# A constant of the feed-forward's last step, added to its rows on another engine and at another time

## The chip, the core and the metric

The kernel runs on one core of a Trainium2 chip. The metric is the device time of one execution in microseconds (us); it was run three times. Five engines matter: TensorE (PE; PEld is its weight load), VectorE (DVE), ScalarE (ACT), GpSimd (POOL) and SyncE (SP), whose queue here issues DMAs. Each engine takes its own instructions in order and waits for the others by semaphores.

## The reference, cut to what matters

The model has two layers of graph attention followed by a feed-forward. The change lies in the feed-forward of the first layer, 30 steps on 4096 rows of 256 channels, whose result is added to the rows it began from:

```python
def step(h, _):
    h = h + 0.01 * jnp.tanh(h)
    h = h * jax.nn.sigmoid(h)
    h = _layernorm(h, ln_w, ln_b)
    h = jnp.einsum('bsc,dc->bsd', h, W) + b
    return (h, None)
...
x = x + _L0_gnn_ref(_layernorm(x, axis=-1), adj, ...)
x = x + _L0_ffn_ref((_layernorm(x, axis=-1))[None], ...)[0]
x = x + _L1_gnn_ref(L1_gnn_t, _layernorm(x, axis=-1), adj, ...)
```

Call the rows before the feed-forward x1 and those after it x2. Then x2 is x1 plus the outcome of the 30th step.

## The kernel before

The 4096 rows are cut into 8 groups (`NG`) of 4 tiles (`G`) of 128 rows. A unit is one step of one group, so there are 240 units (`units`), and the steps of a group follow each other with seven other groups between. Between steps the kernel keeps h times 100 in an SBUF tile `y` [128, 32, 256].

A function `slot(at)` writes one turn of a software pipeline. In slot `at` the engines work on different units:

- `th` of unit `at`: ScalarE's tanh (L826), then GpSimd's add of `y` (L827). The add has an extra wait written by hand: for VectorE's `lower` instruction (L818) of the same slot, with the reason "the port that both use".
- unit `at - 2`: ScalarE's silu into `z` (L815) and the f16 part of half of it (L817); VectorE's rest of that part (L818); a DMA transpose of both f16 parts from SP's queue (L822); VectorE's statistics (L839, L841).
- unit `at - 3`: TensorE's transposes of the other half (L796), ScalarE's copy `zT` (L846), and the inverse deviation `z_rs`, which takes one small ScalarE instruction (L849) and two small GpSimd instructions (L850 with a power of -0.5, L851).
- unit `at - 4`: TensorE's matmuls into `po` (L863 in f32, L866 in f16 parts), two PSUM buffers.
- unit `at - 5`: VectorE's `po` times `z_rs` plus a constant (L803), four instructions of 128 x 256. In steps 1 to 29 the constant is `bias`; in the last it is `last`, made once at the beginning (L730) with the scale for the final result, and the outcome goes to `y` as well.
- also unit `at - 5`, in the last step only: GpSimd adds the group of `y` to the rows x1 (L877, one instruction of 128 x 1024), and SP stores the sum as x2 (L878). The first four groups stay in SBUF for the next stage in `ahead`.

```python
if units - NG <= u < units:
    g = u % NG
    t = x1.pop(g)
    nc.gpsimd.tensor_tensor(t, t, y[:, g * G : (g + 1) * G, :], OP.add)
    nc.sync.dma_start(rows_of(x2d, g), t)
```

The rows x1 are loaded again for this: groups 0 to 3 into the pool `stream` through `load`, groups 4 to 7 into four tiles `x1` of their own (L790).

The order in slots 0 to 239 is kept as written for PE, DVE, ACT and POOL (`manual_schedule`). SP is not among these engines, and the last six slots (240 to 245) and all of the next stage are ordered by the scheduler of the language, by its own estimates. It can put instructions of the next stage between the last written ones where data permits.

The next stage is `attention("g1", ...)`. Its preparation takes each group of x2: row statistics (L100, L102), 1/deviation (L104, L105), transposes (L113), a copy (L271), the products `ph` (L300), which use PSUM that `po` had, and `fs` (L314) in two halves. Groups 4 to 7 are read back from x2 in HBM by SP (L92), into the buffers of groups 0 to 3.

Of the kernel before, what the change touches and what calls it, by code (L numbers as in the profile page):

```python
# [11 lines left out]
F32 = mybir.dt.float32  # L12
# [6 lines left out]
OP = mybir.AluOpType  # L19
# [4 lines left out]
P = 128  # L24
C = 256
# [4 lines left out]
G = 4  # L30
# [16 lines left out]
def gnn_ffn_kernel(ctx: ExitStack, tc: tile.TileContext, a: dict, out: bass.AP):  # L47
    nc = tc.nc
# [3 lines left out]
    NG = NT // G  # L52
# [26 lines left out]
    x1d = dram.tile([N, C], F32, name="x1d")  # L79
    x2d = dram.tile([N, C], F32, name="x2d")  # L80
# [3 lines left out]
    def rows_of(t, g):  # L84
        return t[g * GR : (g + 1) * GR, :].rearrange("(r p) c -> p r c", p=P)

    ahead = {}
    stream = []

    def load_ahead(src, g, view=rows_of, queue=nc.sync):  # L90
        t = stream[-1].tile([P, G, C], F32, name="rows")
        queue.dma_start(t, view(src, g))  # L92
        ahead[g] = t
# [554 lines left out]
    with ExitStack() as scope:  # L648
# [8 lines left out]
        bias = one.tile([P, C], F32, name="bias")  # L657
        last = one.tile([P, C], F32, name="last")
        y = one.tile([P, NT, C], F32, name="y")
        work = scope.enter_context(tc.tile_pool(name="f_work", bufs=3))  # L660
        small = scope.enter_context(tc.tile_pool(name="f_small", bufs=6))

        x1 = {}

        def load(g, queue=nc.sync):
            if g not in ahead:
                load_ahead(x1d, g, queue=queue)
            x1[g] = ahead.pop(g)
# [3 lines left out]
        def measure(g):  # L672
            st = small.tile([P, G, 6], F32, name="x_st")
            mv = measured[g] = small.tile([P, G, 2], F32, name="x_mv")
            for r in range(G):
                nc.vector.bn_stats(st[:, r, :], x1[g][:, r, :])
            for r in range(G):
                nc.vector.bn_aggr(mv[:, r, :], st[:, r, :])

        def rate(g):  # L680

            mv = measured.pop(g)
            rs = small.tile([P, G], F32, name="x_rs")
            nc.scalar.activation(rs, mv[:, :, 1], AF.Identity, scale=1e-4, bias=eps[:, 1:])
            nc.gpsimd.tensor_tensor(rs, rs, mhalf, OP.pow)
            nm = small.tile([P, G], F32, name="x_nm")
            nc.gpsimd.tensor_tensor(nm, mv[:, :, 0], rs, OP.mult)
            nc.gpsimd.tensor_scalar(nm, nm, -1.0, None, op0=OP.mult)
            rates[g] = rs, nm

        def init(g):
            t = x1.pop(g)
            rs, nm = rates.pop(g)
            for r in range(G):
                nc.scalar.activation(
                    y[:, g * G + r, :], t[:, r, :], AF.Identity, scale=rs[:, r : r + 1], bias=nm[:, r : r + 1]
                )
# [83 lines left out]
        units = FFN_STEPS * NG  # L781
        def slot(at):
            if 0 < at and at + 3 < NG:
                load(at + 3)
            g = at - (units - NG - 4)
            if 0 <= g < NG // 2:
                load(g)
            elif NG // 2 <= g < NG:
                x1[g] = work.tile([P, G, C], F32, name="x1", bufs=NG - NG // 2)
                nc.sync.dma_start(x1[g], rows_of(x1d, g))  # L790
            u = at - 3
            if 0 <= u < units:
                z = zs.pop(u)
                pt = ps_t.tile([P, GR], F32, name="tp")
                for r in range(G):
                    nc.tensor.transpose(pt[:, r * P : (r + 1) * P], z[:, r, :P], ident)  # L796
            u = at - 5
            if 0 <= u < units:
                g = u % NG
                po, rstd = pos.pop(u), rs.pop(u)  # L800
                end = u >= units - NG
                for r in range(G):
                    nc.vector.scalar_tensor_tensor(  # L803
                        y[:, g * G + r, :],
                        po[:, r, :],
                        rstd[:, r : r + 1],
                        last if end else bias,
                        op0=OP.mult,
                        op1=OP.add,
                    )  # L810
            u = at - 2
            lower = None
            if 0 <= u < units:
                z = zs[u] = work.tile([P, G, C], F32, name="z")
                nc.scalar.activation(z, th.pop(u), AF.Silu, scale=0.01)  # L815
                z16 = work.tile([P, 2, G, P], F16, name="z16", bufs=4)
                nc.scalar.activation(z16[:, 0], z[:, :, P:], AF.Identity, scale=scale[:, :1])  # L817
                lower = nc.vector.scalar_tensor_tensor(  # L818
                    z16[:, 1], z[:, :, P:], scale[:, :1], z16[:, 0], op0=OP.mult, op1=OP.subtract
                )  # L820
                zT16[u] = work.tile([P, 2 * G, P], F16, name="zT16", bufs=4)
                nc.sync.dma_start_transpose(zT16[u], z16.rearrange("p s r c -> p (s r c)"))  # L822
            if at < units:
                g = at % NG
                th[at] = work.tile([P, G, C], F32, name="th", bufs=4)
                nc.scalar.activation(th[at], y[:, g * G : (g + 1) * G, :], AF.Tanh, scale=0.01)  # L826
                ins = nc.gpsimd.tensor_tensor(th[at], th[at], y[:, g * G : (g + 1) * G, :], OP.add)  # L827
                if lower is not None:
                    tc.add_manual_dep(
                        ins.ins,  # L830
                        lower.ins.name,
                        mybir.DependencyInfo(mybir.DependencyClass.Sync, mybir.DependencyReason.DATA),
                        reason="the port that both use",
                    )
            if 0 <= u < units:
                st = small.tile([P, G, 6], F32, name="z_st")
                mv = small.tile([P, G, 2], F32, name="z_mv")
                for r in range(G):
                    nc.vector.bn_stats(st[:, r, :], z[:, r, :])  # L839
                for r in range(G):  # L840
                    nc.vector.bn_aggr(mv[:, r, :], st[:, r, :])  # L841
                mvs[u] = mv
            u = at - 3
            if 0 <= u < units:
                zT[u] = work.tile([P, GR], F32, name="zT")
                nc.scalar.copy(zT[u], pt)  # L846

                rs[u] = small.tile([P, G], F32, name="z_rs")
                nc.scalar.activation(rs[u], mvs.pop(u)[:, :, 1], AF.Identity, bias=eps[:, :1])  # L849
                nc.gpsimd.tensor_tensor(rs[u], rs[u], mhalf, OP.pow)  # L850
                nc.gpsimd.tensor_tensor(rs[u], rs[u], under[:, int(u >= units - NG), :], OP.mult)  # L851
            if at + 2 < NG:
                rate(at + 2)
            if at + 1 < NG:
                init(at + 1)
            if at + 3 < NG:
                measure(at + 3)
            u = at - 4
            if 0 <= u < units:
                src, src16 = zT.pop(u), zT16.pop(u)  # L860
                po = pos[u] = ps_o.tile([P, G, C], F32, name="po")
                for r in range(G):
                    nc.tensor.matmul(po[:, r, :], src[:, r * P : (r + 1) * P], wT, start=True, stop=False)  # L863
                    for part in range(2):
                        for other in range(2):
                            nc.tensor.matmul(  # L866
                                po[:, r, :],
                                src16[:, part * G + r, :],
                                w16[:, other, :],
                                start=False,  # L870
                                stop=(part == 1 and other == 1),
                            )
            u = at - 5
            if units - NG <= u < units:
                g = u % NG
                t = x1.pop(g)
                nc.gpsimd.tensor_tensor(t, t, y[:, g * G : (g + 1) * G, :], OP.add)  # L877
                nc.sync.dma_start(rows_of(x2d, g), t)  # L878
                if g < NG // 2:
                    ahead[g] = t  # L880

        with tc.manual_schedule(
            engines={
# [9 lines left out]
        for at in range(units, units + 6):  # L893
            slot(at)
# [12 lines left out]
    for i in range(2):  # L907
        at = 1 + i * KC * E
# [29 lines left out]
    with ExitStack() as scope:  # L938
# [253 lines left out]
        with tc.tile_pool(name="r_ps", bufs=1, space=PSUM) as psum, tc.tile_pool(  # L1192
            name="r_pst", bufs=4, space=PSUM
# [19 lines left out]
        work = scope.enter_context(tc.tile_pool(name="m_work", bufs=3))  # L1213
# [166 lines left out]
```

## Time and profile before

| what | us |
|---|---|
| median of 3 runs (lowest, highest) | 3008.34 (3007.27, 3010.92) |
| the profiled run's own time | 3008.46 |
| its span, first to last instruction | 3006.8 |
| mean granted TensorE clock | 0.974 of full |
| GpSimd: 240 adds L827, busy (mean of one) | 568.2 (2.368) |
| GpSimd: 240 L850, busy (mean of one) | 245.7 (1.024) |
| GpSimd: 240 L851, busy (mean of one) | 96.1 (0.400) |
| GpSimd: 8 adds L877, busy | 18.8 |
| VectorE: 32 last-step L803, busy (mean of one) | 15.3 (0.476) |

The feed-forward's first L827 begins at 609.7 us and the last at 1561.7; the 32 last-step L803 begin between 1546.7 and 1581.2. Times in the views count from the first instruction of the execution. An instruction's row may begin some hundredths before its predecessor on the same engine has ended[...]. An idle time in square brackets stands before an instruction, with the engine and line that ended it.

### The profile page before, as it was taken

The numbers are of one execution on the slowest core, as the hardware profiler recorded it, in microseconds if no ns is written. First come the engines' busy times: TensorE is split into PE (matmuls) and PEld (weight loads), VectorE is DVE, ScalarE is ACT, GpSimd is POOL, SyncE is SP. The second block draws the span as 40 slices with busy tenths as digits, with TensorE's granted clock in tenths as the row PEclk, the third lists the DMA queues.
The fourth block names the chain that finished last, engine by engine and source line by source line (L and its number), as shares of the span: only waits on it lengthen the run. The fifth ranks groups of instructions, "written<-read, shape, count | busy, mean of one in ns | idle before, by whom it ended". The sixth has DMA issues, their size and how long they took to land. (4 is left out here: it accounts for less than half of the span.)

```text
span 3006.8 us, 82646 instructions
## 1 busy us (share of the span) xinstructions
PE 2813.1 (94%) x33923; PEld 2568.3 (85%) x33923; DVE 2741.0 (91%) x5766; ACT 2462.0 (82%) x3132; POOL 1173.2 (39%) x1056
## 2 busy tenths in 40 slices
PE   6899999979999999999998999999889999986996
PEld 5799999958888888888876999999789999975996
DVE  8999999989999999999998899999689999986775
ACT  5799999788888888888866999999699999963442
POOL 2000000089999999999993000000200000013663
PEclk9999999989999999999999999999999999997998
DMA  9999784143333333333343031220303132133253
GB/s 292 267 256 249 224 247 118 33 133 70 68 68 67 68 70 69 68 68 68 68 95 121 20 103 51 76 79 27 107 20 93 51 107 79 51 96 123 82 172 134
DMA packets 482899, 320.08 MB, mean 106 GB/s; under 512 B 416573, under 2 KB 443354, under 8 KB 476378
## 3 DMA queue, kind: packets, MB, share of 16 engines
q1 hardware_dynamic: 467698, 287.13, 35.6%
q0 software_dynamic: 7680, 21.51, 2.3%
q10 hardware_dynamic: 7144, 6.16, 0.6%
q8 instruction: 268, 4.39, 0.6%
q14 instruction: 109, 0.89, 0.1%
HBM read 183.00 MB, written 52.04 MB: 78 GB/s over the span
## 5 line engine op out<-in xcount | busy, mean ns | idle before, releaser
L519 PE MATMUL acc<-vals,st 128*128 128x130 f16 x12288 | 1431.1, 218 | 36.1 <-DVE u L472 27.9
L519 PE MATMUL acc<-vals,below 128*128 128x130 f16 x12288 | 1430.7, 221 | 12.6 <-DVE below L573 11.9
L461 ACT ACTIVATE st<-f1b,nf 128x1024 int8<-128x1024 f32 x1265 | 1334.2, 1142 | 29.9 <-PE acc L519 24.6
L519 PEld LDWEIGHTS <-below 128*128 128x128 fp8e4 x12288 | 1175.7, 96 | 49.4 <-issue 44.5
L519 PEld LDWEIGHTS <-st 128*128 128x128 fp8e4 x12288 | 1207.5, 98 | 9.6 <-DVE st L567 7.5
L863 PE MATMUL po<-wT,zT 128*128 128x256 f32 x1920 | 576.1, 382 | 7.4 <-ACT zT L846 7.4
L827 POOL TENSOR_TENSOR th<-th,y 128x1024 f32<-128x1024 f32 x240 | 568.2, 2368 | 27.2 <-ACT th L826 4.4
L866 PE MATMUL po<-w,zT 128*128 128x256 f16 x3840 | 577.9, 273 | 0.3 <-DMA zT<-z 0.3
L866 PEld LDWEIGHTS <-zT 128*128 128x128 f16 x3840 | 376.3, 98 | 161.6 <-DMA zT<-z 1.2
L573 DVE TENSOR_TENSOR below<-m,st 128x1024 int32<-128x1024 int32 x384 | 470.0, 1224 | 32.8 <-DVE st L567 1.3
L567 DVE TENSOR_TENSOR st<-st,m 128x1024 int32<-128x1024 int32 x384 | 467.5, 1217 | 0.2
L803 DVE SCALAR_TENSOR_TENSOR y<-po,z_rs,bias 128x256 f32<-128x256 f32 x928 | 384.4, 477 | 2.1 <-PE tp L796 0.7
L839 DVE BATCH_NORM_STATS2 z_st<-z 128x6 f32<-128x256 f32 x960 | 335.8, 413 | 0.0
L863 PEld LDWEIGHTS po<-wT,zT 128*128 128x128 f32 x1920 | 291.1, 192 | 17.4 <-ACT zT L846 9.0
L105 POOL TENSOR_TENSOR ln_rstd<-ln_rstd,mhalf 128x4 f32<-128x4 f32 x24 | 32.3, 1345 | 586.5 <-ACT acc L1033 491.8
L815 ACT ACTIVATE z<-th 128x1024 f32<-128x1024 f32 x240 | 251.2, 1047 | 8.6 <-POOL th L827 8.3
L826 ACT ACTIVATE th<-y 128x1024 f32<-128x1024 f32 x240 | 249.8, 1041 | 0.1
L850 POOL TENSOR_TENSOR z_rs<-z_rs,mhalf 128x4 f32<-128x4 f32 x240 | 245.7, 1024 | 0.0
L846 ACT COPY zT<-tp 128x512 f32<-128x512 f32 x240 | 140.4, 585 | 110.5 <-PE tp L796 110.4
L459 DVE TENSOR_SCALAR st<-f1b,nf 128x1024 int8<-128x1024 f32 x271 | 201.2, 743 | 8.4 <-PE acc L519 8.4
L436 POOL MEMSET hs<- 128x4 f32 x3 | 0.3, 101 | 491.9 <-DVE u L489 491.9
L818 DVE SCALAR_TENSOR_TENSOR z<-z,scale,z 128x512 f16<-128x512 f32 x240 | 179.4, 747 | 4.9 <-ACT z L817 4.9
(252 smaller groups left out, 2970.2 us busy)
## 6 DMA issues: line engine op xcount, KB each, us to landing
adj<-in_adj_dram SPq DMA_DIRECT2D x64, 1024.0 KB
m<-edges SPq DMA_DIRECT2D x32, 1024.0 KB
f1b<-fd SPq DMA_DIRECT2D x48, 512.0 KB
edges<-m SPq DMA_DIRECT2D x16, 1024.0 KB
y<-yd SPq DMA_DIRECT2D x16, 512.0 KB
ew<-in_L_ffn_expert_w_dram SPq DMA_DIRECT2D x18, 256.0 KB
t<-in_x_dram SPq DMA_DIRECT2D x8, 512.0 KB
old<-in_x_dram SPq DMA_DIRECT2D x16, 256.0 KB
```

The source lines that it names most:

```text
L461: nc.scalar.activation(out, f1, AF.Sign, bias=f2, scale=-1.0)
L519: nc.tensor.matmul(acc[:, i, cols], masked[part][:, at_i // TR, s, rows], v[:, cols], start=(j == 0 and part == 0), stop=(j == NT - 1 and ...
L567: nc.vector.tensor_tensor(above, above, whole, OP.bitwise_and)
L573: nc.vector.tensor_tensor(below, whole, above, OP.bitwise_xor)
L803: nc.vector.scalar_tensor_tensor(y[:, g * G + r, :], po[:, r, :], rstd[:, r : r + 1], last if end else bias, op0=OP.mult, op1=OP.add,)
L815: nc.scalar.activation(z, th.pop(u), AF.Silu, scale=0.01)
L826: nc.scalar.activation(th[at], y[:, g * G : (g + 1) * G, :], AF.Tanh, scale=0.01)
L827: ins = nc.gpsimd.tensor_tensor(th[at], th[at], y[:, g * G : (g + 1) * G, :], OP.add)
L839: nc.vector.bn_stats(st[:, r, :], z[:, r, :])
L850: nc.gpsimd.tensor_tensor(rs[u], rs[u], mhalf, OP.pow)
L863: nc.tensor.matmul(po[:, r, :], src[:, r * P : (r + 1) * P], wT, start=True, stop=False)
L866: nc.tensor.matmul(po[:, r, :], src16[:, part * G + r, :], w16[:, other, :], start=False, stop=(part == 1 and other == 1),)
```

## The change

The constant of the last step no longer comes in with VectorE's last instruction. Instead, GpSimd adds `last` to the rows x1 beforehand, one tile of 128 x 256 at a time, in 32 instructions spread over slots 40 to 220: a group every 24 slots, its four tiles at the 8th, 12th, 16th and 20th of them, each written at the end of a slot behind L851. In the last step VectorE's instruction takes these rows as its addend and writes its result over them. The eight GpSimd adds L877 go away, and the store follows VectorE's instruction directly. The lines that load the rows x1 move to one group every 24 slots from slot 32. `y` isn't written in the last step.

```diff
         def slot(at):
             if 0 < at and at + 3 < NG:
                 load(at + 3)
-            g = at - (units - NG - 4)
-            if 0 <= g < NG // 2:
-                load(g)
-            elif NG // 2 <= g < NG:
-                x1[g] = work.tile([P, G, C], F32, name="x1", bufs=NG - NG // 2)
-                nc.sync.dma_start(x1[g], rows_of(x1d, g))
+            g, part = divmod(at - 4 * NG, 3 * NG)
+            if 0 <= g < NG and part == 0:
+                if g < NG // 2:
+                    load(g)
+                else:
+                    x1[g] = work.tile([P, G, C], F32, name="x1", bufs=NG - NG // 2)
+                    nc.sync.dma_start(x1[g], rows_of(x1d, g))
...
                 end = u >= units - NG
+                t = x1.pop(g) if end else None
                 for r in range(G):
                     nc.vector.scalar_tensor_tensor(
-                        y[:, g * G + r, :],
+                        t[:, r, :] if end else y[:, g * G + r, :],
                         po[:, r, :],
                         rstd[:, r : r + 1],
-                        last if end else bias,
+                        t[:, r, :] if end else bias,
                         op0=OP.mult,
                         op1=OP.add,
                     )
+                if end:
+                    nc.sync.dma_start(rows_of(x2d, g), t)
+                    if g < NG // 2:
+                        ahead[g] = t
...
-            u = at - 5
-            if units - NG <= u < units:
-                g = u % NG
-                t = x1.pop(g)
-                nc.gpsimd.tensor_tensor(t, t, y[:, g * G : (g + 1) * G, :], OP.add)
-                nc.sync.dma_start(rows_of(x2d, g), t)
-                if g < NG // 2:
-                    ahead[g] = t
+            g, part = divmod(at - 4 * NG, 3 * NG)
+            r, part = divmod(part - NG, 4)
+            if 0 <= g < NG and 0 <= r < G and part == 0:
+                nc.gpsimd.tensor_tensor(x1[g][:, r, :], x1[g][:, r, :], last, OP.add)
```

## The prediction

> **What bounds the kernel now.** I read the busy table of stretches first, then the order of time of one ordinary slot of the feed-forward, then the waits and the order of time of its end, and last what other places show of the two engines that share something.
>
> Stretches (columns: stretch, its length, busy us of PE, PEld, DVE, ACT, POOL with counts, granted clock, DMA share, GB/s):
>
> ```profile
> 1000.00:1300.00 300.00, 300.00 (x2146) 245.72 (x2145) 299.14 (x998) 260.19 (x383) 287.32 (x230) 1.00 0.34 68
> 1546.75:1588.60 41.85, 34.93 (x219) 27.02 (x217) 34.45 (x117) 14.61 (x24) 38.34 (x28) 0.96 0.51 150
> ```
>
> In mid-stage TensorE is busy 300 of 300 us at full clock and VectorE 299; GpSimd 287. From the first `last` row to the next stage's start TensorE idles 7 of 42 us, and GpSimd is the busiest engine. So the change puts work where GpSimd has little room, and takes it from where GpSimd leads.
>
> One ordinary slot in order of time (start, us, engine, line):
>
> ```profile
> 1386.90 1.02 POOL L850 TENSOR_TENSOR z_rs<-z_rs,mhalf 128x4 f32<-128x4 f32 x1
> 1387.08 1.05 ACT L815 ACTIVATE z<-th 128x1024 f32<-128x1024 f32 x1
> 1387.61 0.74 DVE L818 SCALAR_TENSOR_TENSOR z<-z,scale,z 128x512 f16<-128x512 f32 x1
> 1388.00 0.40 POOL L851 TENSOR_TENSOR z_rs<-z_rs,under 128x4 f32<-128x4 f32 x1
> 1388.49 2.37 POOL L827 TENSOR_TENSOR th<-th,y 128x1024 f32<-128x1024 f32 x1
> 1390.32 0.59 ACT L846 COPY zT<-tp 128x512 f32<-128x512 f32 x1 [0.49 <-PE tp L796]
> 1390.82 1.01 POOL L850 TENSOR_TENSOR z_rs<-z_rs,mhalf 128x4 f32<-128x4 f32 x1
> 1391.52 0.75 DVE L818 SCALAR_TENSOR_TENSOR z<-z,scale,z 128x512 f16<-128x512 f32 x1
> ```
>
> The period is 1391.52 - 1387.61 = 3.91 us. GpSimd looks full, but L851 ends at 1388.40, just after L818's end (1388.35), and takes 0.40 us where it takes 0.20 beside no L818 (its row below). So about 0.2 us of GpSimd's slot is slack, spent waiting. ScalarE has 0.49 us of its own in front of L846. TensorE has none.
>
> The end of the stage:
>
> ```profile
> 1557.30 0.93 DVE L818 SCALAR_TENSOR_TENSOR z<-z,scale,z 128x512 f16<-128x512 f32 x1
> 1557.64 1.46 POOL L850 TENSOR_TENSOR z_rs<-z_rs,mhalf 128x4 f32<-128x4 f32 x1
> 1559.18 0.20 POOL L851 TENSOR_TENSOR z_rs<-z_rs,under 128x4 f32<-128x4 f32 x1
> 1559.33 2.37 POOL L877 TENSOR_TENSOR rows<-rows,y 128x1024 f32<-128x1024 f32 x1
> ...
> 1564.49 1.06 ACT L815 ACTIVATE z<-th 128x1024 f32<-128x1024 f32 x1 [4.44 <-POOL th L827]
> 1566.07 0.78 PE L863 MATMUL po<-wT,zT 128*128 128x256 f32 x2 [2.59 <-ACT zT L846]
> ...
> 1580.06 1.64 DVE L803 SCALAR_TENSOR_TENSOR y<-po,z_rs,last 128x256 f32<-128x256 f32 x4
> 1581.85 3.80 PE L300 MATMUL ph<-g_w,xT 128*128 128x264 f32 x16 [1.52 <-DVE y L803]
> 1582.98 0.39 SPq L92 DMA_DIRECT2D rows<-x2d  x1
> 1587.27 1.40 DVE L100 BATCH_NORM_STATS2 ln_st<-rows 128x6 f32<-128x256 f32 x4 [3.10 <-DMA rows<-x2d]
> 1588.59 0.16 DVE L314 TENSOR_TENSOR fs<-ph,ln_rstd 128x16 f32<-128x16 f32 x1
> ```
>
> Read it as a chain: the L877 adds hold up GpSimd, so `th` is late, so ScalarE's `z` waits 4.44, so TensorE waits 2.59. Afterwards the queue of SP, held by stores that wait for L877, sends the load of group 4's rows only at 1582.98, and VectorE waits 3.10 for it before the second `fs` of the next stage at 1588.59.
>
> [...]the L818 of 1557.30 ends 0.55 us after the GpSimd add before it (1555.33 + 2.35 = 1557.68), stretched from 0.74 to 0.93; the L850 that came meanwhile took 1.46 for 1.02. [...]here a running L850 (1386.90 to 1387.92) did not hold up L818 at 1387.61[...]. [...]after the 2.59 us gap the trace shows matmuls of 1.06 us where 0.60 is usual[...].
>
> **The change part by part.**
>
> *Removed at the end:* eight L877 of 2.35 us, 18.8 us of GpSimd from 1553.00 to 1585.73. *Unchanged:* VectorE's 32 last-step instructions, same shape and count, one PSUM and one SBUF tensor; I cost the other SBUF tensor (rows instead of `last`) at nothing, since neither read nor write grows; were it dearer, 0.01 us x 32 = 0.3 us. The row loads: SP is not among the engines kept in written order, and the program's order has the loads at the stage's beginning in both kernels (trace: L92 and L790 between 602 and 660 us), so moving their lines moves nothing. The stores keep their places in SP's queue among the transposes, but wait for VectorE instead of GpSimd.
>
> *Added in mid-stage:* 32 adds of 128x256, each behind L851, four slots apart. From below 2.37/4 = 0.59; from above, 0.20 (128x4) + 252 x (2.37 - 0.20)/1020 = 0.74. I take 0.73. Queued behind it is the next L827, and behind that L850; ScalarE's `z` waits for L827. With L818's start as zero, L851 ends at 0.79, the piece may start at 0.76 (such followers start 0.04 before their predecessor's end) and L827 starts at about 1.45 instead of 0.88: late by 0.57. It recovers about 0.21 a slot (L851 no longer waits), so 0.36, 0.15, 0 in the following slots, before the next piece in the fourth. ScalarE's `z` starts at -0.53 and was ready 0.10 earlier, so it is late by about 0.5; the 0.49 in front of L846 takes that up, and zT is needed by TensorE only some 3 us later. L818 works 2.6 us behind its input from ScalarE. So TensorE sees nothing: 0 us, if the port does not bite. It does not if L850, now starting at 3.78, reads before the next L818 (start 3.91) takes the lock. L818 needs 0.74 alone but 0.55 after a lock frees, so it takes it about 0.17 after its start, at 4.08; L850 needs 1.02 alone and 0.87 after a lock frees, so it asks within 0.15 of its start, at 3.93. Margin 0.15 us. I take 0; the ends are -0 (nothing is removed there) and +50, worked out below.
>
> *What the end becomes:* TensorE's period of 3.92 continues from its transposes at 1554.32; five more bring the last unit's matmuls to begin at 1570.0 and end at 1573.5, where before they ended at 1579.2. Transposes of the next stage to 1574.6. VectorE is next: between the last steps it has layer-norm rows of the next stage; summing its rows (after the step of group 6 at 1570.9: 1.64 for it, 2.1 for statistics) the step of group 7 runs 1574.6 to 1576.2, TensorE's L300 starts 1576.35 for 1581.85 (-5.5) and ends 1580.2. Group 4's load can go when the transposes have read group 0's buffer, 1574.7, and lands about 4.2 us later (1582.98 to 1587.27 before), 1579.0; statistics to 1580.4; second `fs` at 1580.5 for 1588.59: -8.1 us. What is late next is equally TensorE's L300 and this load. The mask loads, which now wait for the last store, come earlier by about as much. The next stage's preparation and all behind it hang on this chain, so the shift stays.
>
> Sum: 0 - 8.1, on the profiled run's 3008.46 (span 3006.8) gives 3000.4; the median of the runs shown is 3008.34, so 3000.2. I forecast 3000.3.
>
> **The rivals.**
>
> *A, the likeliest:* gain at the end of 5.5 (only TensorE's start counts) to 10 us (the load lands sooner, clock kept), nothing paid in mid-stage: 2998 to 3003. For it: the 4.44 and 3.10 waits; against it: the next stage's instruction order shifts a little.
>
> *B, leaks:* each piece costs TensorE 0.1 to 0.2 us, because ScalarE's slack of 0.49 is about as large as its delay of 0.5, or L818 is caught briefly: 32 x 0.15 = 4.8, so 3005. For it: three engines are full; against: TensorE's inputs are ready slots ahead.
>
> *C, slower, the lock flips:* if L850 asks after L818 has the lock, it ends 0.87 after L818's end, L851 and L827 follow, and L827 then ends past the next L818's start. That keeps itself up: 0.55 + 0.87 + 0.08 + 0.20 + 0.09 + 2.37 = 4.16 us a slot for GpSimd, while VectorE comes back to L818 earlier, at 3.6 us after the same point, and is caught again. From the first piece (slot 40) to slot 240: 200 x (4.16 - 3.92) = 48, less 8: 3048. It decides from a delay of about 0.72 us instead of my 0.57, that is a piece of 0.88 us. For it: 1.46 and 2.80 us rows at the end show the lock; against: the margin, and the upper bound of 0.74.
>
> **How the numbers follow.** A 0.68, B 0.18, C 0.14. A measurement of this kernel tells about 0.2% (6 us) from no change: faster is below 3002.3. Of A about nine tenths lie there (0.61) and the rest is same; B is mostly same (0.16) with 0.01 each side; C slower, one part in ten lighter and short-lived. Faster 0.62, same 0.22, slower 0.16. The range leaves out C and the lowest of A: 2997 to 3009; A's own is 2998 to 3003.5.
>
> **What would show it.** Right: 32 GpSimd adds of 0.6 to 0.75 us; L827's waiters nil; TensorE still 300 of 300 in mid-stage; periods of 3.92; no 4.44 and 2.59 waits at the end; second `fs` about 8 us earlier against the stage's last ordinary slot. Wrong: mid-stage periods above 3.92, L850 at 1.4 us or L818 above 0.9 in many slots (C), ScalarE or TensorE waiting for `th` behind each piece (B), or a load that lands as late as before.

## The result and the profile after

| | before | after |
|---|---|---|
| median, us (7 runs each) | 3006.16 | 2997.61 |
| lowest to highest, us | 3005.27 to 3010.92 | 2994.00 to 3003.10 |

The ratio is 0.9970, with a 95% interval of 0.9960 to 0.9979: 8.55 us faster, against 8.1 us predicted (the interval is 6.3 to 12.0 us). The median was forecast as 3000.3; 2.2 of the 2.7 us between are the kernel before, whose median of seven runs is 3006.16 and of the first three 3008.34. The profiled run of after happens to be the longest of its seven (3003.1 us). Its feed-forward begins 5.15 us later than the one profiled before: the last matmul L519 of the stage ahead starts at 603.29, before at 598.14. What lies ahead of that point differs between executions of every kernel (597.2 to 603.3 for that matmul in the profiles here), so below times are compared from a point in the stage. Lines after L784 have other numbers in the new program: L796 has become L797, L818 L824, L827 L833, L850 L856, L851 L857, L803 L805, L815 L821, L846 L852, L863 L869, L866 L872; a piece of the new work is L882.

First the stretches of after (start and end, length, then busy us of PE, PEld, DVE, ACT, POOL, granted clock, DMA share, GB/s): a piece of mid-stage, and the 41.84 us from the first last-step row on.

```profile
1000.00:1300.00 300.00, 300.00 (x2145) 245.72 (x2143) 299.18 (x994) 263.17 (x385) 289.54 (x245) 1.00 0.34 68
1551.90:1593.74 41.84, 39.48 (x259) 32.00 (x257) 37.74 (x132) 21.77 (x34) 22.08 (x26) 1.00 0.73 211
```

TensorE is still busy 300 of 300 us in mid-stage, with GpSimd at 289.54 instead of 287.32. At the stage's end GpSimd has fallen from 38.34 to 22.08 us, and TensorE rises from 34.93 to 39.48 in a stretch of the same length, at a granted clock of 1.00 instead of 0.96.

Then the waits of after between 700 and 1546 us (sum, times, longest):

```profile
ACT zT L852 <- PE tp L797: 85.4, 183, 0.5
ACT z L821 <- POOL th L833: 11.8, 35, 0.6
DVE y L805 <- PE tp L797: 0.7, 2, 0.4
```

In the kernel before, the first of these was:

```profile
ACT zT L846 <- PE tp L796: 105.0, 216, 0.5
```

TensorE is missing from the list of after. The pieces show up as ScalarE's 35 waits for `th`, 0.34 us each on average; they vanish in the 0.5 us that ScalarE otherwise waits in front of L852, 183 times now and 216 times before.

One piece in order of time (start, us, engine, line; only the rows of VectorE, GpSimd and ScalarE that matter):

```profile
785.16 0.74 DVE L824 SCALAR_TENSOR_TENSOR z<-z,scale,z 128x512 f16<-128x512 f32 x1
...
785.92 0.72 POOL L882 TENSOR_TENSOR rows<-rows,last 128x256 f32<-128x256 f32 x1
...
786.60 2.36 POOL L833 TENSOR_TENSOR th<-th,y 128x1024 f32<-128x1024 f32 x1
...
788.93 1.01 POOL L856 TENSOR_TENSOR z_rs<-z_rs,mhalf 128x4 f32<-128x4 f32 x1
...
789.00 1.06 ACT L821 ACTIVATE z<-th 128x1024 f32<-128x1024 f32 x1 [0.34 <-POOL th L833]
789.08 0.74 DVE L824 SCALAR_TENSOR_TENSOR z<-z,scale,z 128x512 f16<-128x512 f32 x1
...
790.17 2.38 POOL L833 TENSOR_TENSOR th<-th,y 128x1024 f32<-128x1024 f32 x1
...
793.00 0.74 DVE L824 SCALAR_TENSOR_TENSOR z<-z,scale,z 128x512 f16<-128x512 f32 x1
...
793.89 2.36 POOL L833 TENSOR_TENSOR th<-th,y 128x1024 f32<-128x1024 f32 x1
```

From L824 to L833 it takes 1.44 us where it took 0.88 before; in the next slots 1.09 and 0.89. So the piece delays GpSimd by 0.56, and two slots later nothing is left of that. The number that decides is that L856 starts at 788.93, 0.15 us ahead of L824, and both keep their ordinary lengths, 1.01 and 0.74 us; the experiments below show the lengths when L856 starts behind.

The end of the stage in after:

```profile
1578.91 1.66 DVE L805 SCALAR_TENSOR_TENSOR x<-po,z_rs,x 128x256 f32<-128x256 f32 x4
1579.70 0.36 SPq L92 DMA_DIRECT2D rows<-x2d  x1
...
1580.94 3.73 PE L300 MATMUL ph<-g_w,xT 128*128 128x264 f32 x16
...
1583.81 1.41 DVE L100 BATCH_NORM_STATS2 ln_st<-rows 128x6 f32<-128x256 f32 x4 [0.61 <-DMA rows<-x2d]
...
1585.13 0.16 DVE L314 TENSOR_TENSOR fs<-ph,ln_rstd 128x16 f32<-128x16 f32 x1
```

ScalarE's wait of 4.44 for `th` is down to at most 1.45, and TensorE's of 2.59 is gone. The load for group 4 leaves at 1579.70, and VectorE waits 0.61 for it instead of 3.10. Counted from the first last-step row (1546.75 before, 1551.90 after), TensorE's L300 starts 29.04 us later instead of 35.10, and the second `fs` 33.23 instead of 41.84: 6.06 and 8.61 us earlier. At a line further on (L433 of the next stage, 88.2 against 97.15) the shift is still 9 us.

### The profile page after: what moved, and what is told of

Its sections match the earlier page's. It is cut to its first block, busy times and chain, and to the rows that moved or that the text cites. A ratio compares the mean times of both kernels' runs of the same rounds, so it can differ in the third digit from the quotient of the medians.

```text
span 3001.4 us, 82666 instructions
## 1 busy us (share of the span) xinstructions
PE 2812.5 (94%) x33923; PEld 2569.1 (86%) x33923; DVE 2737.4 (91%) x5766; ACT 2469.0 (82%) x3132; POOL 1161.5 (39%) x1080
## 5 line engine op out<-in xcount | busy, mean ns | idle before, releaser
L519 PE MATMUL acc<-vals,st 128*128 128x130 f16 x12288 | 1434.6, 219 | 36.1 <-DVE u L472 27.5
L519 PE MATMUL acc<-vals,below 128*128 128x130 f16 x12288 | 1434.2, 221 | 12.4 <-DVE below L573 11.9
L519 PEld LDWEIGHTS <-below 128*128 128x128 fp8e4 x12288 | 1177.6, 96 | 48.8 <-issue 43.8
L519 PEld LDWEIGHTS <-st 128*128 128x128 fp8e4 x12288 | 1209.3, 98 | 10.0 <-DVE st L567 7.5
L869 PE MATMUL po<-wT,zT 128*128 128x256 f32 x1920 | 574.8, 381 | 4.7 <-ACT zT L852 3.4
L872 PE MATMUL po<-w,zT 128*128 128x256 f16 x3840 | 576.8, 273 | 0.0
L833 POOL TENSOR_TENSOR th<-th,y 128x1024 f32<-128x1024 f32 x240 | 567.2, 2363 | 21.7 <-ACT th L832 4.4
L872 PEld LDWEIGHTS <-zT 128*128 128x128 f16 x3840 | 376.2, 98 | 160.1 <-issue 0.6
L805 DVE SCALAR_TENSOR_TENSOR y<-po,z_rs,bias 128x256 f32<-128x256 f32 x928 | 384.5, 477 | 2.1 <-PE tp L797 0.7
L869 PEld LDWEIGHTS po<-wT,zT 128*128 128x128 f32 x1920 | 290.4, 191 | 14.0 <-ACT zT L852 5.8
L821 ACT ACTIVATE z<-th 128x1024 f32<-128x1024 f32 x240 | 251.8, 1049 | 15.2 <-POOL th L833 14.9
L856 POOL TENSOR_TENSOR z_rs<-z_rs,mhalf 128x4 f32<-128x4 f32 x240 | 244.1, 1017 | 3.1 <-ACT z_rs L855 3.1
L852 ACT COPY zT<-tp 128x512 f32<-128x512 f32 x240 | 140.5, 585 | 90.8 <-PE tp L797 89.5
L824 DVE SCALAR_TENSOR_TENSOR z<-z,scale,z 128x512 f16<-128x512 f32 x240 | 178.4, 743 | 4.9 <-ACT z L823 4.9
```

The lines of the kernel that those rows point to most:

```text
L519: nc.tensor.matmul(acc[:, i, cols], masked[part][:, at_i // TR, s, rows], v[:, cols], start=(j == 0 and part == 0), stop=(j == NT - 1 and ...
L805: nc.vector.scalar_tensor_tensor(t[:, r, :] if end else y[:, g * G + r, :], po[:, r, :], rstd[:, r : r + 1], t[:, r, :] if end else bias, ...
L872: nc.tensor.matmul(po[:, r, :], src16[:, part * G + r, :], w16[:, other, :], start=False, stop=(part == 1 and other == 1),)
```

## The experiments

Two theories stood at first. *End:* GpSimd's eight adds at the end were the whole cost, and the 32 pieces are free. *Leak:* the pieces cost a little in mid-stage, and the end gains more than is seen. A third, the prediction's rival C, is about what the pieces could have cost: the *lock*, which keeps itself up once L856 comes too late. The word is the prediction's. What the rows of before show is that an L818 begun while an L827 runs takes longer (0.93 us at 1557.30 instead of 0.74), and an L850 begun beside that L818 too (1.46 instead of 1.02); what in the chip does it, no run shows. In what follows "lock" stands for these longer times, and slots are "caught" when they run in the longer rhythm that comes with them. "Stage" is the time from the first L833 (L827 before) to the first last-step row, 937.02 us before and after.

### Only the pieces, only the end

The kernel before with the 32 pieces added, its end as it was (the constant is added twice). The lines that load the rows move as in after; that part is left out here:

```diff
...
+            g, part = divmod(at - 4 * NG, 3 * NG)
+            r, part = divmod(part - NG, 4)
+            if 0 <= g < NG and 0 <= r < G and part == 0:
+                nc.gpsimd.tensor_tensor(x1[g][:, r, :], x1[g][:, r, :], last, OP.add)
```

> The kernel before, with the 32 mid-stage adds put in as well; its end is untouched, so the constant of the last step is added twice. My theory (mid-stage adds are free, the gain is all at the end): same as before within 2 us, about 3006; TensorE busy 300 of 300 us in mid-stage, slots of 3.92 us, from the first L827 to the first last-step row about 937.0 us as in both kernels; second fs about 41.8 us after the first last-step row. Rival that the adds cost TensorE 0.1 to 0.2 us each: 3009 to 3012 and a stage longer by 3 to 6 us. Rival that the gain comes from the mid-stage: below 3003.

Measured: 3007.20 us (14 runs) beside 3006.96, ratio 1.0000 (0.9992 to 1.0008); stage 937.02 us.

The kernel after without the pieces (the constant is left out):

```diff
-            g, part = divmod(at - 4 * NG, 3 * NG)
-            r, part = divmod(part - NG, 4)
-            if 0 <= g < NG and 0 <= r < G and part == 0:
-                nc.gpsimd.tensor_tensor(x1[g][:, r, :], x1[g][:, r, :], last, OP.add)
```

> The changed kernel without the 32 mid-stage adds: the constant of the last step is left out of the result. My theory: as the changed kernel, 2997.6 within 2 us, second fs 33.2 us after the first last-step row. Rival that the mid-stage adds cost a little that the end pays for: 2 to 6 us below the changed kernel, 2992 to 2996, with a stage shorter by as much.

Measured: 2999.35 us (10 runs), ratio 0.9977 (0.9968 to 0.9986); stage 937.01; L300 29.04 us and the second `fs` 33.09 us behind the first last-step row, as in after. The two halves agree: the pieces cost nothing, within 0.02 us of stage time, and the whole gain is at the end. The leak is out.

### GpSimd at the end, or the path of the data

The old adds also held up the stores. To split the two, the kernel after got eight GpSimd adds of 128 x 1024 in the old places, into a tile that nobody reads; the stores still follow VectorE.

```diff
+        spare = one.tile([P, G, C], F32, name="spare")
+        done = {}
...
+                    done[g] = t
...
+            u = at - 5
+            if units - NG <= u < units:
+                g = u % NG
+                nc.gpsimd.tensor_tensor(spare, done.pop(g), y[:, g * G : (g + 1) * G, :], OP.add)
```

> The changed kernel with eight GpSimd adds of 128x1024 put back at the places of the old L877, into a spare tile that nobody reads: GpSimd is as occupied at the end as before, but stores and statistics don't wait for it. If the gain is GpSimd's time in front of th (late th, late z, late zT, TensorE idle): most of it goes, second fs at 38 to 40 us after the first last-step row (before 41.8, after 33.2), about 3003 to 3004. Rival that the gain is that stores and statistics no longer wait for the sum: second fs stays at 33 to 35 us, 2998 to 2999.

Measured: 3006.36 us (14 runs), ratio 0.9999 (0.9991 to 1.0007). Its end in order of time (L889 is the idle add, L836 the old L827, L824 here ScalarE's `z`, L872 TensorE's `po`):

```profile
1559.82 2.36 POOL L889 TENSOR_TENSOR spare<-rows,y 128x1024 f32<-128x1024 f32 x1
...
1571.31 1.06 ACT L824 ACTIVATE z<-th 128x1024 f32<-128x1024 f32 x1 [4.44 <-POOL th L836]
...
1573.08 1.22 PE L872 MATMUL po<-wT,zT 128*128 128x256 f32 x2 [2.78 <-ACT zT L855]
...
1588.70 3.83 PE L300 MATMUL ph<-g_w,xT 128*128 128x264 f32 x16 [0.51 <-DVE x L807]
1588.73 1.36 DVE L100 BATCH_NORM_STATS2 ln_st<-rows 128x6 f32<-128x256 f32 x4
...
1592.57 0.17 DVE L314 TENSOR_TENSOR fs<-ph,ln_rstd 128x16 f32<-128x16 f32 x1 [0.20 <-PE ph L300]
```

The waits of before are back, 4.44 of ScalarE and 2.78 of TensorE, although nobody needs the result. From the first last-step row (1553.37) L300 takes 35.33 us, as before (35.10): eight adds on GpSimd bring back all of TensorE's 6.06 us. (They take GpSimd's time and, like the old ones, make VectorE's `z` longer: the L827 of 1562.86 takes 2.18 us instead of 0.74, begun while an L836 runs that ends at 1564.49; this run doesn't part the two.) But L100 no longer waits for a load, and the second `fs` comes after 39.20 instead of 41.84: 2.64 of the 8.61 us belong to the stores that no longer wait for GpSimd. The time itself can't be used as a measure of this split: with the added tile and work the scheduler put the stage's preparation in another order, and from the last L519 of the stage ahead to the first L827 (here VectorE's `z`) it takes 26.03 us instead of 23.60; with a first slot of 4.80 instead of 4.26 that makes 3.0 us lost ahead of what was to be tested. Without them it would be 3003.4, an estimate.

### Larger pieces: does the lock flip, and does it stay?

Eight adds of 128 x 1024 instead of the 32 pieces, one for each group, 24 slots apart:

```diff
...
-            r, part = divmod(part - NG, 4)
-            if 0 <= g < NG and 0 <= r < G and part == 0:
-                nc.gpsimd.tensor_tensor(x1[g][:, r, :], x1[g][:, r, :], last, OP.add)
+            if 0 <= g < NG and part == NG:
+                nc.gpsimd.tensor_tensor(x1[g], x1[g], last[:, None, :].to_broadcast([P, G, C]), OP.add)
```

> The changed kernel with the constant added in eight instructions of 128x1024 instead of 32 of 128x256, each about 2.4 us, at the place of a group's first piece. Theory of the lock that keeps itself up once an add is longer than 0.88 us: from the first one on L833 ends after the next L824 has started, L856 takes 1.4 us and L824 over 0.9 in nearly every slot, slots of 4.16 us until the stage's end, 3035 to 3045. Rival that GpSimd gets back in step by itself within some slots because of 0.2 us of slack in each: only single slots show it, at most 2 us for each add, 2998 to 3014, with L824 back at 0.74 before the next add.

Measured: 3032.35 us (5 runs), ratio 1.0088 (1.0075 to 1.0101); stage 974.4, 37.3 us longer. That is 3 us less than expected: no slot of 4.16 us is there, the lasting ones take 4.02. To see whether that is one lasting state or eight separate disturbances, only one such add was kept, in slot 40 (the constant is left out of the other groups; the edit is against the run above):

```diff
-            g, part = divmod(at - 4 * NG, 3 * NG)
-            if 0 <= g < NG and part == NG:
-                nc.gpsimd.tensor_tensor(x1[g], x1[g], last[:, None, :].to_broadcast([P, G, C]), OP.add)
+            if at == 5 * NG:
+                nc.gpsimd.tensor_tensor(x1[0], x1[0], last[:, None, :].to_broadcast([P, G, C]), OP.add)
```

> After without the pieces, but with a single add of 128 x 1024 (group 0) in slot 40; the constant is left out of the other seven groups, so only one disturbance is in the stage. If the lock's phase keeps itself up, the slots stay at about 4.02 us to the end of the stage from this one add on: 200 x 0.10 = 20 us and about 2 for the add itself, so 3019 to 3023. Rival, the whole adds cost because each new one catches the slots behind it and the phase heals before the next: one eighth of the 37 us, 4 to 5 us, so 3002 to 3005, with slots back at 3.91 within 24.

Measured: 3015.87 us (5 runs), ratio 1.0034 (1.0020 to 1.0048); the stage is 21.2 us longer. The time lies 3 us below its range although the stage grew as expected: what lies outside the stage varies by as much. The order of time around the one add (L880):

```profile
779.02 0.74 DVE L824 SCALAR_TENSOR_TENSOR z<-z,scale,z 128x512 f16<-128x512 f32 x1
...
779.78 2.36 POOL L880 TENSOR_TENSOR rows<-rows,last 128x1024 f32<-128x1024 f32 x1
...
782.10 2.35 POOL L833 TENSOR_TENSOR th<-th,y 128x1024 f32<-128x1024 f32 x1
...
782.94 2.06 DVE L824 SCALAR_TENSOR_TENSOR z<-z,scale,z 128x512 f16<-128x512 f32 x1
...
784.41 1.47 POOL L856 TENSOR_TENSOR z_rs<-z_rs,mhalf 128x4 f32<-128x4 f32 x1
...
786.10 2.36 POOL L833 TENSOR_TENSOR th<-th,y 128x1024 f32<-128x1024 f32 x1
...
788.06 0.96 DVE L824 SCALAR_TENSOR_TENSOR z<-z,scale,z 128x512 f16<-128x512 f32 x1
...
788.43 1.46 POOL L856 TENSOR_TENSOR z_rs<-z_rs,mhalf 128x4 f32<-128x4 f32 x1
...
789.97 0.20 POOL L857 TENSOR_TENSOR z_rs<-z_rs,under 128x4 f32<-128x4 f32 x1
790.12 2.37 POOL L833 TENSOR_TENSOR th<-th,y 128x1024 f32<-128x1024 f32 x1
...
792.08 0.96 DVE L824 SCALAR_TENSOR_TENSOR z<-z,scale,z 128x512 f16<-128x512 f32 x1
```

L824 starts at 782.94 while GpSimd's add L833 runs, and ends 0.55 us after it (784.45, so 785.00): it takes 2.06 us instead of 0.74. L856, begun meanwhile, takes 1.47 us instead of 1.02. From then on each slot repeats this. L824 (788.06) runs into the tail of L833 (786.10 + 2.36 = 788.46) and takes 0.96; L856, begun 0.37 us behind L824, takes 1.46 and ends 0.87 us after it; L833 is late again. The slots are 4.02 us apart instead of 3.92, for 192 slots up to the stage's end, and nothing heals, though the cause was a single instruction. The rival (an eighth of 37 us) is out.

### Where it flips

Sixteen adds of 128 x 512, eight slots apart within a group, and 24 adds of 128 x 340 or 344, five slots apart. Both take the place of the 32 pieces, whose lines are left out here:

```diff
...
+            r, part = divmod(part - NG, 8)
+            if 0 <= g < NG and 0 <= r < 2 and part == 0:
+                two = x1[g][:, 2 * r : 2 * r + 2, :]
+                nc.gpsimd.tensor_tensor(two, two, last[:, None, :].to_broadcast([P, 2, C]), OP.add)
```

> After, with the constant added in 16 adds of 128 x 512 (about 1.25 us each, estimated from 0.72 for 128 x 256 and 2.37 for 128 x 1024) in slots 40, 48 and so on up to 216. Lock theory, with the prediction's threshold of a piece of 0.88 us: the first of them is enough, slots from slot 40 on are of about 4.02 us as with the whole adds (not 3.91), L856 at 1.4 us and L824 at 0.96, the stage is longer by at least 200 x 0.10 = 20 us, at most the 37 of the eight whole adds: 3018 to 3035. Rival, the phase only flips behind a delay near the length of half a slot: the pieces are made up for within eight slots (0.21 a slot), the stage stays at 937 us and the time at 2997 to 3003.

```diff
...
+            r, part = divmod(part - NG, 5)
+            if 0 <= g < NG and 0 <= r < 3 and part == 0:
+                cols = slice((0, 85, 170, 256)[r], (0, 85, 170, 256)[r + 1])
+                some = x1[g][:, :, cols]
+                nc.gpsimd.tensor_tensor(some, some, last[:, None, cols].to_broadcast([P, G, some.shape[2]]), OP.add)
```

> After, with the constant added in 24 adds of 128 x 340 or 344 (four rows' tiles of 85 or 86 columns in one instruction), estimated at 0.90 us each, five slots apart. The prediction put the point at which the port lock flips at a piece of 0.88 us, so this is just past it. Lock theory with that point: slots of 4.02 us from the first piece on, the stage longer by 20 us or a little more, 3017 to 3025. The same theory with a threshold put too low: no slot changes, stage 937 us, 2997 to 3003. A leak without a flip would be seen as an idle TensorE behind each piece: 24 x 0.1 to 0.2 = 2.4 to 5 us.

Measured: the sixteen, 1.28 us each, 3037.47 us (4 runs), ratio 1.0103 (1.0086 to 1.0120), stage 38.9 us longer: caught from the first piece on, and 2 us above what was expected. The 24, 0.92 us each, 3017.35 us in the median of 19 runs, ratio 1.0032 (1.0015 to 1.0049), but from 3004.71 to 3037.73. Two pieces of this one profile, 39 us apart:

```profile
781.27 0.91 POOL L884 TENSOR_TENSOR rows<-rows,last 128x340 f32<-128x340 f32 x1
...
784.43 0.78 DVE L824 SCALAR_TENSOR_TENSOR z<-z,scale,z 128x512 f16<-128x512 f32 x1
784.47 1.02 POOL L856 TENSOR_TENSOR z_rs<-z_rs,mhalf 128x4 f32<-128x4 f32 x1
...
820.47 0.92 POOL L884 TENSOR_TENSOR rows<-rows,last 128x344 f32<-128x344 f32 x1
...
823.63 0.74 DVE L824 SCALAR_TENSOR_TENSOR z<-z,scale,z 128x512 f16<-128x512 f32 x1
823.67 1.59 POOL L856 TENSOR_TENSOR z_rs<-z_rs,mhalf 128x4 f32<-128x4 f32 x1
...
827.55 0.85 DVE L824 SCALAR_TENSOR_TENSOR z<-z,scale,z 128x512 f16<-128x512 f32 x1
```

Nearly the same contest, ended in both ways: L856 starts 0.04 us behind L824 each time. At 784.47 it keeps its 1.02 us (L824 is stretched from 0.74 to 0.78) and the delay heals; at 823.67 L824 keeps its 0.74, L856 takes 1.59, and the slots stay at 4.02 us to the end. So 0.92 us is the edge. Chance between executions shows in the 19 times: by the sizes below, an execution is 5 us shorter for each group of pieces that passes before one is caught. Within this profile chance isn't shown, since the piece that was caught is four elements longer than the two that passed (the other passed in slot 45). Once caught, GpSimd has no slack left, and every later piece costs nearly its length: a slot with a piece of 0.92 is 4.89 us long (0.87 more), one with 1.28 is 5.24 (1.22 more). That gives the sizes: 195 slots x 0.103 (4.023 less 3.920) and 15 x 1.22 make 38.4 of the 38.9 us that the sixteen added.

The 24 once more:

> The 24 adds of 128 x 340 or 344 once more, to see a second execution. Its runs lay between 3004.7 and 3037.7. Lock theory: some piece catches the slots, in another place than in the first profile (slot 50), and from there every slot is of 4.02 us and every later piece costs 0.87: the stage is longer than 937 us by 0.10 x (240 - s) + 0.87 for each piece after slot s, whatever s is, and no slot ahead of s is longer. Rival, slots are lost here and there over the whole stage and heal again.

Measured: one run of 3043.11 us, on a chip where the kernel before took 3022.89. It was caught at the same third piece (slot 50, the first one of 344 elements), not at another, while those of 340 in slots 40 and 45 passed, with L856 0.04 and 0.03 us behind L824; ahead of it no slot is longer, behind it 160 slots of 4.02 us and 21 of 4.89. The stage grew by 37.3 us, where the same sum, 183 slots x 0.103 and 21 x 0.87, gives 37.1.

### A piece below the edge, and a slot that is not like the others

Twenty-four pieces of 128 x 300 (0.82 us), with eight of the 124 elements that are left (0.44 us), should have been safe. The edit is against the run with 24 adds:

```diff
...
             r, part = divmod(part - NG, 5)
-            if 0 <= g < NG and 0 <= r < 3 and part == 0:
-                cols = slice((0, 85, 170, 256)[r], (0, 85, 170, 256)[r + 1])
+            if 0 <= g < NG and 0 <= r < 4 and part == 0:
+                cols = slice((0, 75, 150, 225)[r], (75, 150, 225, 256)[r])
```

> After, with the constant added in 32 adds, 24 of 128 x 300 and 8 of 128 x 124, five slots apart. A piece of 300 elements should take 0.82 us (0.724 for 256 and 0.918 for 342 measured). In the run with pieces of 0.91 and 0.92 us L856 began 0.04 us behind L824 and won once and lost once, so a piece has to be below about 0.91; with 0.82 L856 begins about 0.05 ahead of L824 and should win each time. Lock theory with that point (0.91, the prediction had 0.88): no slot is caught, stage 937 us, 2997 to 3003, with a spread of runs like that of after. Rival, the point lies lower or the outcome is chance over a wide band: some runs are caught, times spread up to 3035.

Measured: 3025.05 us (12 runs) beside 3022.89, ratio 1.0006 (0.9998 to 1.0015), with runs within 6 us of each other. Sixteen long pieces and five short ones passed; the one of slot 165 was caught in the profile, and the stage grew by 13.8 us:

```profile
1260.50 0.74 DVE L824 SCALAR_TENSOR_TENSOR z<-z,scale,z 128x512 f16<-128x512 f32 x1
...
1264.79 0.74 DVE L824 SCALAR_TENSOR_TENSOR z<-z,scale,z 128x512 f16<-128x512 f32 x1
...
1268.59 0.75 DVE L824 SCALAR_TENSOR_TENSOR z<-z,scale,z 128x512 f16<-128x512 f32 x1
...
1272.38 0.75 DVE L824 SCALAR_TENSOR_TENSOR z<-z,scale,z 128x512 f16<-128x512 f32 x1
...
1273.15 0.82 POOL L884 TENSOR_TENSOR x<-x,last 128x300 f32<-128x300 f32 x1
...
1276.18 0.75 DVE L824 SCALAR_TENSOR_TENSOR z<-z,scale,z 128x512 f16<-128x512 f32 x1
1276.26 1.54 POOL L856 TENSOR_TENSOR z_rs<-z_rs,mhalf 128x4 f32<-128x4 f32 x1
...
1280.10 0.85 DVE L824 SCALAR_TENSOR_TENSOR z<-z,scale,z 128x512 f16<-128x512 f32 x1
```

The starts of L824 tell why: 1260.50, 1264.79, 1268.59, 1272.38, 1276.18, that is one slot of 4.29 and then three of 3.80, in which VectorE catches up. In each of the three it begins L824 0.12 us earlier, and L856 is 0.08 behind it instead of 0.03 to 0.06 ahead, as behind the long pieces of other slots. The same 4.29 and 3.80 stand at the same place in the kernel before and in after. What VectorE waits for there can be read in the kernel before:

```profile
1260.96 1.66 DVE L803 SCALAR_TENSOR_TENSOR y<-po,z_rs,bias 128x256 f32<-128x256 f32 x4 [0.37 <-PE tp L796]
```

The wait of 0.37 us ends with TensorE's transposes, which this instruction doesn't read. Between 700 and 1546 us that happens only here and 128 slots earlier: these are the two waits of `y` for `tp` in the list of after above. Why only there is open. So the pieces of this group were moved out of the way, to slots 168, 172, 176 and 180:

```diff
-            g, part = divmod(at - 4 * NG, 3 * NG)
-            r, part = divmod(part - NG, 5)
-            if 0 <= g < NG and 0 <= r < 4 and part == 0:
+            for g in range(NG):
+                r, part = divmod(at - (5 + 3 * g + (g == 5)) * NG, 4 if g == 5 else 5)
+                if 0 <= r < 4 and part == 0:
```

> As e8 (24 adds of 128 x 300 and 8 of 128 x 124), but the pieces of group 5 in slots 168, 172, 176 and 180 instead of 160, 165, 170 and 175, so that none falls into the slots 162 to 165. There every kernel's profile, the one before too, shows one slot of 4.29 us and then three of 3.80, in which VectorE catches up and comes to L824 0.12 us earlier each time; in e8 the piece of slot 165 (0.83 us) was the one that caught. If that coincidence is the cause, no slot is caught now: stage 937 us, no slot of 4.02, and against before a ratio like that of after, 0.997 (0.9960 to 0.9979). If 0.82 us is too long in itself, slots of 4.02 appear elsewhere and the ratio stays at 1.0006.

> The changed kernel once more, beside e10 on the same chip. In its first profile the piece of slot 164 (0.73 us) let L856 begin only 0.03 us ahead of L824, 0.07 short of the point at which e6 was caught, and escaped. Theory: 0.73 stays on the safe side, stage 937 us, ratio 0.997, and e10 the same within its interval. If that slot is caught in some executions, those lose 76 x 0.10 + 12 x 0.70 = 16 us, and its times fall into two groups 16 us apart.

Measured: 3014.68 us for the shifted pieces and 3016.04 for after (5 runs each), beside 3027.51; ratios 0.9959 (0.9945 to 0.9973) and 0.9964 (0.9949 to 0.9979). (On these chips the kernel before takes 16 to 20 us more than on the others; the stage of after is as long there as here.) No slot of either is 4.02 us long; over slots 40 to 235 both take 768.32 us, as does the kernel before (768.32). Four pieces out of 32, moved to other slots, are worth the whole loss of 13.8 us in the stage. Against after the shifted ones gain nothing: the intervals overlap, and the stage is the same. And after itself, in this second profile, is close at its own piece of slot 164:

```profile
1266.97 0.73 DVE L824 SCALAR_TENSOR_TENSOR z<-z,scale,z 128x512 f16<-128x512 f32 x1
...
1267.72 0.72 POOL L882 TENSOR_TENSOR x<-x,last 128x256 f32<-128x256 f32 x1
...
1270.73 1.02 POOL L856 TENSOR_TENSOR z_rs<-z_rs,mhalf 128x4 f32<-128x4 f32 x1
1270.77 0.73 DVE L824 SCALAR_TENSOR_TENSOR z<-z,scale,z 128x512 f16<-128x512 f32 x1
```

L856 is ahead of L824 by 0.04 us only, where the other pieces have about 0.15. It escapes in both profiles.

## Why the prediction was right

- **The end.** L300 was put 5.5 us earlier and came 6.06 earlier; the second `fs` 8.1, and came 8.61. VectorE's step of group 7 was put at 1574.6; less the later beginning of 5.15 us it starts at 1573.8, and that is the difference. The load, put at 1574.7, leaves at 1574.6 on the same count; VectorE takes its rows up at 1578.7, for the 1579.0 put. That TensorE's L300 and this load are about equally late next was right: 0.61 us of waiting for the load are left. That the medians differ by 8.55, so close to 8.1, is partly luck: the interval is 6 us wide, and in the two profiled runs what follows the first last-step row is 10.5 us shorter. It is the 6.06 and 8.61 in the order of time that bear the forecast out.
- **Who held up what.** The chain "GpSimd's adds, so `th`, so `z`, so TensorE" was right for all of L300's shift, and "stores hold the queue" for a further 2.6 us: the idle adds brought the first back and not the second.
- **The pieces.** 0.73 us was assumed, 0.72 measured; a delay of 0.57, measured 0.56; the recovery of 0.21 a slot was too low, it is 0.35 (1.44, 1.09 us from L824 to L833, and 0.89 in the slot after that, where nothing is left to recover). TensorE sees nothing. Case B, leaks of 0.1 to 0.2 us a piece, would be 3 to 6 us of stage; there are under 0.05. That VectorE's last-step instruction would cost the same with rows as addend was right within the 0.01 us allowed (0.473 before, 0.476 after).
- **The lock (case C).** What the prediction took from rows of the stage's end came back in mid-stage with the same sizes: in the run with one add the L824 of 782.94 is 1.3 us longer than usual and ends 0.55 us after GpSimd's L833, and the L856 of 788.43 ends 0.87 us after L824. The point was nearly right too: a piece of 0.88 us, measured 0.92. Two terms were mis-sized. The slow slot was put at 4.16 us and is 4.02: the sum took 0.09 us between L857 (then L851) and the next add, as in an ordinary slot, and in a caught slot the add starts 0.05 before L857's end (789.97 + 0.20, then 790.12). That is 0.14 x 200 = 28 of the 48 us; the single whole add gave 21. And the cost of every later piece by its length was left out, which is why sixteen or 24 larger pieces lose 37 to 39 us all the same.
- **The margin.** The prediction had L856 start 0.13 us ahead of L824, and the flip at 0.02 behind, an estimate from the 0.74, 0.55, 1.02 and 0.87 us of its rows: a margin of 0.15. In ordinary slots L856 is 0.15 ahead, and the flip comes at about 0.04 behind: 0.19. The step that failed is to take one ordinary slot for all 200. In slot 164 VectorE is catching up, and there the lead is 0.03 to 0.04; the change stayed clear of case C by some 0.07 us.

The chances given add to 0.15 at most for slower and to 0.23 for same, not 0.16 and 0.22.

Of the expectations, those of the 24 pieces of 300 elements (caught after all, in slot 165), of the second profile of the 340s (same slot, not another), and of the idle adds' time missed, the last for the preparation's order. The times of the eight whole adds, of the single one and of the sixteen lie outside their ranges too, by 2 to 3 us, and of the 24 the median lies inside and the single runs don't. Why those two profiles were caught in the same slot while 19 runs spread over 33 us stays open (the piece there is the first of 344 elements); so does why VectorE waits for the transposes in two slots and in no other.

## What to carry to other kernels

Work that waits at a stage's end for its last input can often be done beforehand on its other operand; what it was worth there is read from who waits behind it, and here adds without a reader held TensorE up as long as those with one. On a nearly full engine cut it into pieces whose delay is made up for before the next piece comes, and work out the margin in the worst slot of the loop, not in a typical one: look through all periods of the stage for the few that differ. If an instruction takes longer when it starts behind another engine's, as L824 behind L833 (0.96 us for 0.74) and L856 behind L824 (1.46 for 1.02) here, ask in a loop without slack what happens after one missed turn; here it never healed, and a single 2.4 us instruction cost 21 us.

## What was not expected of the hardware

- VectorE and GpSimd, each in a fixed order, have two steady rhythms in this stage: 3.92 and 4.02 us a slot; in the second L824 takes about 0.96 us and L856 about 1.47 (medians in the run with eight whole adds), for 0.74 and 1.02 in the first. One instruction switches to the second, and nothing in 190 slots switched back.
- When GpSimd's L856 starts 0.03 to 0.05 us behind VectorE's L824, either outcome is possible: of six such contests in two profiles four passed, and the two that followed the first piece of 344 elements were caught (L856 took 1.59 us in the first profile). From execution to execution the outcome differs: with 24 such contests a program's time spreads over 33 us, where the kernel before spreads over 9.
- Two slots, 128 apart (the 34th and the 162nd, counted from one L824 to the next), are 4.27 and 4.29 us long in the kernels before and after, because VectorE waits 0.36 and 0.37 us for transposes there. With the idle adds they stand at the 68th and the 196th (so not in every kernel at the same place, as one expectation has it), and 32 more instructions on GpSimd don't move them. So the place changes with the program; what sets it is open.
